# Cross-attention with sparsemax and a two-branch feed-forward: row normalisation on ScalarE, the 32-row tile's queries on column tiles, first loads from two queues, split relus, and a new emission order

## The chip, the cores and the metric

The kernel runs on one core of a Trainium2 chip. A core has TensorE (PE, matrix products; PEld is its weight load), VectorE (DVE), ScalarE (ACT), GpSimd (POOL) and SyncE (SP, which here only issues transfers). The engines run side by side, each through its own list of instructions in order, and wait for each other at semaphores. The metric is the device time of one execution in microseconds. The profile is of one further execution.

## The reference

Eight batches; each has 100 query rows of 512 numbers and a context of 722 rows. All is float32.

```
h   = layernorm(x)
q,k,v = h @ Wq + bq, ctx @ Wk + bk, ctx @ Wv + bv      # 16 heads of 32
s   = q k^T / sqrt(32)
att = sparsemax(s)          # max(s - tau, 0), with tau such that a row sums to 1
x   = x + (att v) @ Wo + bo
h2  = layernorm(x)
out = x + sqrt((h2 @ cos(theta + theta_noise))^2 + (h2 @ sin(phi + phi_noise))^2)
```

## The kernel before, in words

**Tiles.** The 800 query rows are cut into seven row tiles, `TILES = (128, 128, 128, 32, 128, 128, 128)`, across batch borders. The context comes transposed, 128 features by 722 positions, four slices a batch. Each float32 matmul stands in the trace as two records, so four matmuls are eight records.

**One batch.** Keys are four groups of 128 by 722, in halves of 361 columns (`keys`, L717; for batch 0 `keys_part`, L706, which works slice by slice as the loads come). ACT adds the bias (L728). A row tile is normalised: `stats` and `deviation` (L518 to L524), `normed` (L528, L530), transposed on PE (L538), copied (L544); `queries` (L554) makes q, four blocks of four matmuls. Scores are made in five fills of the one wide PSUM tile `psc` (`fill`, L800, on 32x32 array tiles; leftovers of four rows, L789, on column tiles). ACT copies each fill to SBUF (L811, two buffers `s_t`). DVE takes the eight largest of every segment of about 30 numbers (`tops`, L822, 312 MAX8 a batch), then builds 80 candidates per row (L831 to L849) and a first bound of the threshold (L857 to L879). Five Newton steps follow: a mask on DVE (`above`, L889), its product with the candidates on GpSimd (`above_values`, L894), a count and a sum on DVE (L900, L907, L908). GpSimd splits the threshold into three bfloat16 parts (`parts`, L929 to L946), PE transposes them (`parts_T`, L951), and `weights` (L995, L1008) makes q k minus the threshold again, transposed, five blocks a batch in the same `psc`. A relu (L1027, ACT; one half of one block on DVE, L1029) writes `aT`, and `outputs` (L1042, column tiles) multiplies with the values (`values`, L738; the last 82 rows L754, on column tiles). ACT adds the bias (L1056).

**A row tile's end.** When all rows of a tile have outputs: product with Wo (`product`, L612; for the last tile one product part per 128 features, L623; for the 32-row tile `small_product`, L580, which spreads the 512 columns over four column tiles), addition to x (L669), normalisation again, two products with the cosine and sine matrices (L612, L580; for the last tile in two column parts of 352 and 160, L638), squares and roots on ACT, sum and result on GpSimd (for the last tile on DVE, L655 and L663), store. GpSimd computes the angles (L488 to L502) during the first batches.

**Order.** The order on every engine is written out by a planner inside the kernel (class `Plan`). Each step is a task with an engine and a cost from the table `STEPS`; `hold` says which buffer a task takes and which tasks free it (`psc` one, `pm` four PSUM banks, `s` two, `x` three). `Plan.order` runs through the tasks as a list scheduler: on each engine the ready task that can start first, among those the one with the earliest due time. A due time is batch x `PERIOD` + `SHIFT` minus the length of the work behind it, plus `LAG` by kind and `NUDGE` by kind and batch; these are tables of numbers. On PE a task of the same array shape as the last is preferred by `STAY`. The tasks are then emitted in order of their planned start.

**Loads.** SP issues all loads, in plan order: first Wk and context slices in pairs, then x, Wq and the rest. 32 small matmuls (`warm_up`, L512) run on PE before the first load is in.

## Time and profile before

| | us |
|---|---|
| median of 3 runs (lowest, highest) | 591.64 (591.51, 592.07) |
| the profiled execution | 594.34 |
| its span, first to last instruction | 592.6 |
| PE busy | 580.5 |
| DVE busy | 517.3 |
| ACT busy | 261.8 |
| POOL busy | 224.2 |
| mean granted PE clock | 0.995 |
| PE waiting for the last row normalisation's copy, at 579.76 | 0.68 |

In the page, the digits of "PE", "DVE" and so on are the busy tenths of forty slices of 14.8 us. "PEclk" is the clock that the array was granted. In a row of a group, what follows the first bar is the busy time in sum and the mean of one in nanoseconds, and what follows the second is the engine's idle time just before, with what ended it. In the rows in order of time, the first number is the start, the second the length, and a bracket holds an idle time and what ended it.

### The profile page before, as it was taken

The numbers are of one execution on the slowest core, as the hardware profiler recorded it, in microseconds if no ns is written. First come the engines' busy times: TensorE is split into PE (matmuls) and PEld (weight loads), VectorE is DVE, ScalarE is ACT, GpSimd is POOL, SyncE is SP. The second block draws the span as 40 slices with busy tenths as digits, with TensorE's granted clock in tenths as the row PEclk, the third lists the DMA queues.
The fourth block names the chain that finished last, engine by engine and source line by source line (L and its number), as shares of the span: only waits on it lengthen the run. The fifth ranks groups of instructions, "written<-read, shape, count | busy, mean of one in ns | idle before, by whom it ended". The sixth has DMA issues, their size and how long they took to land.

```text
span 592.6 us, 18085 instructions
## 1 busy us (share of the span) xinstructions
PE 580.5 (98%) x6937; PEld 339.1 (57%) x6937; DVE 517.3 (87%) x3186; ACT 261.8 (44%) x399; POOL 224.2 (38%) x293
## 2 busy tenths in 40 slices
PE   9999999999999999999999999999999999999995
PEld 6655554567456743677457744576557544664553
DVE  3299999998999879998999899999999899999521
ACT  1353352455346523654345434363545534552532
POOL 1686799974400232004620232015200446045402
PEclk9999999999999989999999999999999999999999
DMA  8940300310011000200100002030000001000001
GB/s 323 316 136 20 118 19 19 108 49 2 19 35 70 2 1 2 102 3 20 43 2 3 2 2 101 3 102 2 3 2 2 14 25 59 3 20 1 3 2 39
DMA packets 12475, 26.61 MB, mean 45 GB/s; under 512 B 1872, under 2 KB 2128, under 8 KB 12384
## 3 DMA queue, kind: packets, MB, share of 16 engines
q1 hardware_dynamic: 11952, 24.03, 12.4%
q8 instruction: 56, 0.92, 0.6%
q0 software_dynamic: 432, 1.38, 0.6%
q14 instruction: 35, 0.29, 0.2%
HBM read 23.76 MB, written 1.64 MB: 43 GB/s over the span
## 4 chain that ended last, share of the span: by engine, by line
PE 60%; DVE 32%; POOL 4%; ACT 2%; issue 1%; DVEq 0%; POOLq 0%; ACTq 0%
PE pm L717 18%; DVE cand L822 15%; PE pm L738 10%; PE psc L1008 5%; PE pm L612 5%; PE pm L1042 4%; PE psc L800 4%; PE pm L554 3%; DVE f L907 3%; DVE m L889 3%; POOL p L894 2%; DVE n L900 2%; PE pm L754 2%; PE psc L706 2%; PE psc L995 2%; DVE rest L831 1%
## 5 line engine op out<-in xcount | busy, mean ns | idle before, releaser
L822 DVE MAX8 cand<-s_t 128x8 f32<-128x30 f32 x2496 | 230.7, 171 | 1.4 <-ACT s_t L811 1.4
L894 POOL TENSOR_TENSOR p<-z,m 128x1040 f32<-128x1040 f32 (+2 forms) x50 | 88.7, 1778 | 266.7 <-DVE m L889 261.8
L717 PE MATMUL pm<-c_t,wk_sb 128*128 128x361 f32 x464 | 152.5, 474 | 0.0
L738 PE MATMUL pm<-wv_sb,c_t 128*128 128x512 f32 x320 | 144.3, 598 | 0.0
L717 PEld LDWEIGHTS pm<-c_t,wk_sb 128*128 128x128 f32 x464 | 84.1, 189 | 53.8 <-issue 10.8
L738 PEld LDWEIGHTS pm<-wv_sb,c_t 128*128 128x128 f32 x320 | 58.5, 190 | 66.7 <-issue 65.6
L811 ACT COPY s_t<-psc 128x1924 f32<-128x1924 f32 (+2 forms) x40 | 69.1, 1726 | 50.1 <-DVE cand L822 30.0
L1027 ACT ACTIVATE aT<-psc 128x2000 f32<-128x2000 f32 (+2 forms) x38 | 66.5, 1749 | 53.2 <-PE pm L1042 36.2
L767 ACT COPY v_t<-pm 128x512 f32<-128x512 f32 x40 | 23.4, 586 | 85.1 <-PE pm L738 85.1
L907 DVE TENSOR_REDUCE f<-p 128x13 f32<-128x1040 f32 (+2 forms) x50 | 50.4, 1009 | 10.6 <-POOL p L894 10.5
L728 ACT ACTIVATE k_t<-pm,bk_sb 128x361 f32<-128x361 f32 x60 | 33.5, 562 | 55.8 <-PE pm L717 55.7
L900 DVE TENSOR_REDUCE n<-m 128x13 f32<-128x1040 bf16 (+2 forms) x50 | 50.3, 1007 | 0.6
L1008 PE MATMUL psc<-q_t,k_t 32*128 32x100 f32 (+1 forms) x1536 | 47.4, 264 | 0.0
L1008 PEld LDWEIGHTS psc<-q_t,k_t 32*128 32x128 f32 (+1 forms) x1536 | 46.4, 180 | 0.4
L800 PE MATMUL psc<-k_t,q_t 32*32 32x481 f32 (+1 forms) x1536 | 43.3, 474 | 0.8 <-ACT s_t L811 0.7
L1042 PE MATMUL pm<-aT,v_t 128*32 128x100 f32 (+1 forms) x1440 | 39.2, 251 | 0.1
L1042 PEld LDWEIGHTS pm<-aT,v_t 128*32 128x32 f32 (+1 forms) x1440 | 30.9, 109 | 7.1 <-issue 3.3
L554 PEld LDWEIGHTS pm<-hT,wq_sb 128*128 128x128 f32 x224 | 27.1, 191 | 6.3 <-issue 5.4
L554 PE MATMUL pm<-hT,wq_sb 128*128 128x128 f32 (+1 forms) x224 | 29.6, 280 | 0.0
L800 PEld LDWEIGHTS psc<-k_t,q_t 32*32 32x32 f32 x1536 | 14.0, 103 | 26.2 <-issue 19.4
L754 PE MATMUL pm<-wv_sb,c_t 128*18 128x128 f32 (+1 forms) x384 | 23.6, 311 | 0.0
L831 DVE MAX8 rest<-cand 128x8 f32<-128x120 f32 x104 | 20.1, 268 | 0.2
(307 smaller groups left out, 615.6 us busy)
## 6 DMA issues: line engine op xcount, KB each, us to landing
c_t<-in_ctx SPq DMA_DIRECT2D x7, 1444.0 KB, 6.6
x_t<-in_x SPq DMA_DIRECT2D x12, 256.0 KB, 3.1
c_t<-in_ctx SPq DMA_DIRECT2D x4, 361.0 KB, 5.1
out<-sq POOLq DMA_DIRECT2D x5, 256.0 KB, 2.8
wk_sb<-in_L_xattn_Wk SPq DMA_DIRECT2D x4, 256.0 KB, 4.6
wq_sb<-in_L_xattn_Wq SPq DMA_DIRECT2D x4, 256.0 KB, 5.7
cos_sb<-in_L_ffn_theta SPq DMA_DIRECT2D x4, 256.0 KB, 4.5
n_t<-in_L_ffn_theta_noise SPq DMA_DIRECT2D x4, 256.0 KB, 3.1
```

Source lines behind the costliest of these rows:

```text
L554: nc.tensor.matmul(tk["pq"][:, g, : tk["n"]], lhsT=wq_sb[:, c, g * P : (g + 1) * P], rhs=tk["hT"][:, c, :], start=(c == 0), stop=(c == NG ...
L717: nc.tensor.matmul(pk, lhsT=wk_sb[:, c, g * P : (g + 1) * P], rhs=st["c"][:, c, i * SH : (i + 1) * SH], start=(c == 0), stop=(c == NG - 1),)
L738: nc.tensor.matmul(pv, lhsT=st["c"][:, k, c * CK : (c + 1) * CK], rhs=wv_sb[:, k, :], start=(k == 0), stop=(k == NG - 1),)
L800: nc.tensor.matmul(psc[b * HD : (b + 1) * HD, j, at : at + EDGE[hi] - EDGE[lo]], lhsT=st["q"][r, g, qb * HD : (qb + 1) * HD], rhs=st["k"][ ...
L811: nc.scalar.copy(s_t[:, :, :n], st["psc"][:, :, :n])
L822: nc.vector.max(st["cand"][:, n, k, :], st["s", f][:, j, at + EDGE[k] - first : at + EDGE[k + 1] - first],)
L894: nc.gpsimd.tensor_tensor(st["p"][:, lo:hi], st["z"][:, lo:hi], st["m"][:, lo:hi], ALU.mult)
L900: nc.vector.tensor_reduce(n_t, st["m"][:, lo:hi], AX.X, ALU.add)
L907: nc.vector.tensor_reduce(s_t, st["p"][:, lo:hi], AX.X, ALU.add)
L1008: nc.tensor.matmul(psc[:m, j, k * Q : (k + 1) * Q], lhsT=st["k"][r, g, lo : lo + m], rhs=st["q"][r, g, :], start=False, stop=(k == len(PAI ...
L1027: nc.scalar.activation(a, b, AF.Relu, scale=SCALE)
L1042: nc.tensor.matmul(st["po", g][j * HD : (j + 1) * HD, :Q], lhsT=st["v"][:m, c, f : f + HD], rhs=aT[j][:m, j, k * Q : (k + 1) * Q], start=( ...
```

## The change

Five things change in what is computed where. (1) `normed` no longer runs on DVE: DVE keeps the reciprocal (`inverse`), ACT negates the mean, multiplies it by the reciprocal and writes the rows with one activation that scales and shifts. (2) The 32-row tile's queries are made by `small_product` on column tiles, copied into columns of its x tile, and turned by one transpose. (3) The first pair of loads is cut in four, weights issued by ACT and context by SP; the keys of the first slice run the first half of the context before the second; the bias bo is loaded early (its due time, in the tables). (4) In the last batch every relu is split, two heads on ACT and two on DVE, into two buffers. (5) The last 160 columns' addition runs on GpSimd. Twelve warm-up matmuls fewer. The losses are computed ahead of the first bound. The planner's costs and rules change a little, and its tables `SHIFT`, `LAG` and `NUDGE` are other numbers (left out here), so that the order on all engines is another.

In the order that results, PE has between two blocks of weights, in most batches, first a key block and then the outputs, where before most often the outputs came first and then the key block; the leftovers' fill stands inside the weights of the batch before in several batches; and the products with the cosine and sine matrices of the last tile but one stand between the last output product and the last normalisation.

```diff
-WARM = 32
+WARM = 20
...
-    "load x": ("SP", 0.7),
+    "load x": ("SP", 0.85),
+    "load first": ("SP", 1.3),
-    "deviation": ("ACT", 0.25),
-    "normed": ("DVE", 0.72),
+    "deviation": ("ACT", 0.45),
+    "inverse": ("DVE", 0.12),
+    "normed": ("ACT", 0.85),
...
+    "small queries": ("PE", 0.95),
+    "small copy": ("ACT", 0.33),
+    "small T": ("PE", 0.15),
...
+    "last result": ("POOL", 0.1, 0.0026),
...
-SHAPE = {"fill": 1, "fill last": 2, "outputs": 2, "small product": 2, "values last": 2, "weights": 3}
+SHAPE = {"fill": 1, "fill last": 2, "outputs": 2, "small product": 2, "small queries": 2, "values last": 2, "weights": 3}
-STAY = 70.0
+STAY = 145.0
+STAY_TILED = 50.0
-PERIOD = 121.0
+PERIOD = 126.0
...
-    LATENCY = {"PE": 0.25, "SP": 2.0}
+    LATENCY = {"PE": 0.25, "SP": 2.6}
...
                 for t in waiting:
...
-                        stay = STAY if engine == "PE" and t.shape == shape else 0.0
+                        stay = 0.0
+                        if engine == "PE":
+                            stay = STAY if t.shape == shape else STAY_TILED if t.shape and shape else 0.0
...
-                late = self.LATENCY.get(t.engine, 0.2)
-                n.ready = max(n.ready, t.end + (0.0 if n.engine == t.engine == "SP" else late))
+                late = 0.0 if n.engine == t.engine else self.LATENCY.get(t.engine, 0.2)
+                n.ready = max(n.ready, t.end + late)
...
-        x_t = rows.tile([P, DM], FP, name="x_t", bufs=3)[:n]
-        nc.sync.dma_start(x_t, rows_of_x)
+        x_t = rows.tile([P, DM], FP, name="x_t", bufs=3)
+        nc.sync.dma_start(x_t[:n], rows_of_x)
...
+    def load_first(st, b):
+
+        st["c"] = big.tile([P, NG, S], FP, name="c_t")
+        for i in range(2):
+            w_cols = slice(P, DM) if i else slice(0, P)
+            nc.scalar.dma_start(wk_sb[:, 0, w_cols], wk[:P, w_cols])
+            keys_i = slice(i * SH, (i + 1) * SH)
+            nc.sync.dma_start(st["c"][:, 0, keys_i], ctxT[b, :P, keys_i])
+
     def load_pair(st, b, c):
-        if c == 0:
-            st["c"] = big.tile([P, NG, S], FP, name="c_t")
...
+        nc.scalar.activation(tk["mv"][:, 0:1], tk["mv"][:, 0:1], AF.Copy, scale=-1.0)
+
+    def inverse(tk):
+        tk["rs"] = small.tile([P, 1], FP, name="rs")[: tk["n"]]
+        nc.vector.reciprocal(tk["rs"], tk["sd"])
     def normed(tk):
-        rs = small.tile([P, 1], FP, name="rs")[: tk["n"]]
-        nc.vector.reciprocal(rs, tk["sd"])
+        shift = tk["mv"][:, 0:1]
+        nc.scalar.activation(shift, shift, AF.Copy, scale=tk["rs"])
...
-        nc.vector.tensor_scalar(
-            tk["h"], tk["x"], tk["mv"][:, 0:1], rs, ALU.subtract, ALU.mult
-        )
+        nc.scalar.activation(tk["h"], tk["x"], AF.Identity, bias=shift, scale=tk["rs"])
...
+    def small_copy(tk):
+        tk["qs"] = tk["x whole"][:, :P]
+        nc.scalar.copy(tk["qs"], tk["pq"])
+
+    def small_T(tk):
+
+        pt = ps1.tile([P, NG, P], FP, name="pm")
+        nc.tensor.transpose(pt[:, 0, :], tk["qs"], ident)
+        tk["pq"] = pt[:, 0, :].rearrange("p (g t) -> p g t", g=NG)
+
     def small_residual(tk):
...
-    def half_result(tk, h):
+    def half_result(tk, h, engine):
...
-        nc.vector.tensor_tensor(a, a, tk["x"][:, half_of(h)], ALU.add)
+        engine.tensor_tensor(a, a, tk["x"][:, half_of(h)], ALU.add)
...
-        for n in range(EARLY):
-            g, i = divmod(n, 2)
+        for i, g in sorted((n % 2, n // 2) for n in range(EARLY)):
...
-    def once(fn):
-        return add("load bias", fn)
-
     def set_x(tk):
...
-        tk["x"] = load_x(x.rearrange("b q d -> (b q) d")[at : at + n], n)
+        tk["x whole"] = load_x(x.rearrange("b q d -> (b q) d")[at : at + n], n)
+        tk["x"] = tk["x whole"][:n]
...
-        h = add("normed" + two, lambda: normed(tk), d)
+        i = add("inverse", lambda: inverse(tk), d)
+        h = add("normed" + two, lambda: normed(tk), i)
...
-        hold("x", tk["x in"], [h])
-        qs = [add("queries", lambda g=g: queries(tk, g), hT, *w["q"]) for g in range(NG)]
-        hold("hT", hT_in, qs)
-        for g in range(1, NG):
-            plan.edge(qs[g - 1], qs[g])
+        if tk["n"] == HD:
+            pq = add("small queries", lambda: small_product(tk, "pq", "hT", wq_sb), hT, *w["q"])
+            cp = add("small copy", lambda: small_copy(tk), pq)
+            qs = [add("small T", lambda: small_T(tk), cp)]
+            hold("hT", hT_in, [pq])
+            hold("pm", pq, [cp])
+            hold("x", tk["x in"], qs)
+        else:
+            hold("x", tk["x in"], [h])
+            qs = [add("queries", lambda g=g: queries(tk, g), hT, *w["q"]) for g in range(NG)]
+            hold("hT", hT_in, qs)
+        for before, q in zip(qs, qs[1:]):
+            plan.edge(before, q)
...
-        tk["q first"] = qs[0]
+        tk["q first"] = pq if tk["n"] == HD else qs[0]
...
-            rz = add("half result", lambda h=h: half_result(tk, h), rt, tiles=z - a)
+            rz = add(
+                "last result" if h else "half result",
+                lambda h=h: half_result(tk, h, nc.gpsimd if h else nc.vector), rt, tiles=z - a,
+            )
...
-            for c in range(NG):
+            c_in.append(add("load first", lambda st=st, b=b: load_first(st, b)))
+            for c in range(1, NG):
...
-            w["bk"] = once(lambda: nc.sync.dma_start(bk_sb, bk))
+            w["bk"] = add("load bias", lambda: nc.sync.dma_start(bk_sb, bk))
...
-            w["bq"] = once(lambda: nc.sync.dma_start(bq_sb, bq))
-            w["bo"] = once(lambda: nc.sync.dma_start(bo_sb, bo.partition_broadcast(P)))
+            w["bq"] = add("load bias", lambda: nc.sync.dma_start(bq_sb, bq))
+            w["bo"] = add("load bo", lambda: nc.sync.dma_start(bo_sb, bo.partition_broadcast(P)))
...
-            w["bv"] = once(lambda: nc.sync.dma_start(bv_sb, bv.rearrange("(g p) -> p g", p=P)))
+            w["bv"] = add("load bv", lambda: nc.sync.dma_start(bv_sb, bv.rearrange("(g p) -> p g", p=P)))
         else:
...
-        for lo, hi in ((0, HG + 1), (HG + 1, 2 * HG + 1), (2 * HG + 1, NT)) if b == B - 1 else ((0, NT),):
+        spans = ((0, HG + 1), (HG + 1, 2 * HG + 1), (2 * HG + 1, NT)) if b == B - 1 else ((0, NT),)
+        for lo, hi in spans:
...
-            t = add("first bound", lambda st=st, r=r: first_bound(st, **r), cd, tiles=hi - lo)
...
+            if hi == NT:
+                ls = add("losses", lambda st=st: losses(st), *cds, *rest_steps)
+            t = add(
+                "first bound", lambda st=st, r=r: first_bound(st, **r), cd, *([ls] if hi == NT else ()),
+                tiles=hi - lo,
+            )
...
-            if b == B - 1 and n == len(PAIRS) - 1:
+            if b == B - 1:
...
-                            st, n, not k, slice(0, 2) if k else slice(2, HG), k
+                            st, n, (n + k) % 2 == 0, slice(0, 2) if k else slice(2, HG), k
...
-                        f, tiles=len(pairs),
+                        f, *top_steps, tiles=len(pairs),
...
-                    for k in (True, False)
+                    for k in (1, 0)
...
-                takes = {"aT": es[0], "s": es[1]}
+                takes = {"aT": es[n % 2], "s": es[1 - n % 2]}
             else:
-                spare = b == B - 1 and n % 2 == 1
-                es = [
-                    add(
-                        "weights relu", lambda st=st, n=n, spare=spare: weights_relu(st, n, spare), f,
-                        *(top_steps if spare else ()), tiles=len(pairs),
-                    )
-                ]
-                takes = {"s" if spare else "aT": es[0]}
+                es = [add("weights relu", lambda st=st, n=n: weights_relu(st, n), f, tiles=len(pairs))]
+                takes = {"aT": es[0]}
             hold("psc", f, es)
```

## The prediction

> **What bounds the kernel now.** I read the page first (busy shares, slices), then the chain that ended last, then TensorE alone in order of time, then the groups by shape.
>
> ```profile
> PE 580.5 (98%) x6937; PEld 339.1 (57%) x6937; DVE 517.3 (87%) x3186; ACT 261.8 (44%) x399; POOL 224.2 (38%) x293
> ...
> PE   9999999999999999999999999999999999999995
> ...
> PEclk9999999999999989999999999999999999999999
> ...
> PE 60%; DVE 32%; POOL 4%; ACT 2%; issue 1%; DVEq 0%; POOLq 0%; ACTq 0%
> ```
>
> TensorE (PE) is never free from 4.8 us, when the keys begin, to 587. Only less work for it, fewer waits or a better clock can shorten the span. The chain runs through VectorE (DVE) for a third of the time because DVE hands each batch's threshold over just in time: before the transposes of batches 0 and 6 PE stood 0.12 and 0.31 us, and in batch 1 the last part was ready 0.29 us ahead. So DVE is a second bound, close behind. The start, from the chain, columns start, length, what:
>
> ```profile
> 1.19 3.60 PE pm L512 x32
> 4.79 3.69 PE psc L706 x8
> ...
> 9.69 2.43 PE psc L706 x8
> ```
>
> The warm-up fills PE until 4.6 us; the first key slice and weights land at 3.71 and 4.65. Eight key records first take 3.69 us, later 2.43: until 6.9 us a record starts every 0.605 us, afterwards every 0.305. The array runs at half speed there, though the page's clock row does not show it. One later stretch, PE in order of time, then the granted clock of three windows (length, PE busy, PEclk, DMA, GB/s):
>
> ```profile
> 204.46 1.97 PE L554 MATMUL pm<-hT,wq_sb 128*128 128x32 f32 x16
> 206.36 0.90 PE L1042 MATMUL pm<-aT,v_t 128*32 128x100 f32 x32
> 207.19 1.08 PE L554 MATMUL pm<-hT,wq_sb 128*128 128x32 f32 x8
> 208.10 5.38 PE L612 MATMUL pm<-wo_sb,oT 128*128 128x512 f32 x8
> 213.32 0.97 PE L554 MATMUL pm<-hT,wq_sb 128*128 128x32 f32 x8
> ```
>
> ```profile
> 204.50:208.20 3.70, 3.70 (x61) 1.00 0.00 0
> 208.25:211.66 3.41, 3.41 (x6) 0.50 0.00 0
> ```
>
> The product at 208.10 takes 5.21 us to the next block; the same eight records take 3.44 elsewhere. It is no wait: the clock was halved for 3.41 us, just after the queries of the 32-row tile. Last, the places where PE waits near the end:
>
> ```profile
> 545.50 0.29 PE L951 MATMUL pm<-ident_b,t 128*128 128x128 bf16 x2 [1.14 <-POOL t L944]
> 558.74 1.07 PE L1042 MATMUL pm<-s_t,v_t 82*32 82x100 f32 x40 [1.16 <-ACT s_t L1027]
> 569.02 0.35 PE L995 MATMUL psc<-tT,neg_b 3*128 3x400 bf16 x4 [0.97 <-ACT s_t L1027]
> 579.76 2.63 PE L638 MATMUL pm<-cos_sb,hT 128*128 128x352 f32 x8 [0.68 <-ACT hT L544]
> ```
>
> With 0.70 at 94.7 us and small ones, PE's waits from 4.79 to 579.76 are 5.3 us.
>
> **The change part by part.** Each is priced on PE's path in the profiled execution (span 592.6 us, 594.34 with what lies around it). That execution is 2.7 us over the median of the runs, 591.64, so I subtract differences from the median.
>
> *Small queries on column tiles.* Removed: the four 32-column blocks, 1.90 + 0.91 + 0.81 = 3.62 us by their starts. Added: one small product, of which the trace has three (0.90, 0.99, 1.01), so 1.0; and one 128x128 transpose, a quarter of a 0.43 to 0.49 block of four, 0.11, with its drain 0.2. The copy between (128x128 on ScalarE, 0.26) lies beside a key block of 2.43 us. Net -2.4.
>
> *The clock dip.* The Trainium skill (TensorE: Matmul & The Clock Gate, What's actually happening) says that a monitor grants the clock by activity over free-running windows of 3.41 us. The dip lasted 3.41, and a window ending at 208.25 held mostly 32-column matmuls. By the row the change saves 5.21 - 3.44 = 1.77; by the rule the phase of the windows is chance, so runs without profile may not have had the dip, and the saving is 0. I take half, -0.9. The same rule speaks against the shorter warm-up: 20 matmuls at 0.107 end at 3.4 us, and if the pause until data arrives counts as idle, full speed comes a window later: 3.41 x 0.5 = 1.7 us lost. The old pause of 0.23 us did no harm; I take 0 and keep 1.7 for the range.
>
> *Start.* The first pair of loads becomes four, on SyncE and ScalarE at once. A 256 KB load issued at 0.88 landed at 3.71; the first needed parts (128 weight columns, half a context slice, 249 KB) should land alike, so keys begin at about 3.85, 0.94 earlier. If full speed still comes at 6.9, (6.9 - 3.85) / 0.605 = 5 records are slow rather than 3.5, and 1.5 x 0.3 = 0.45 goes back. Net -0.5, ends 0 and -0.95. The bo load (256 KB) now precedes pair 1, which landed at 6.99; at the 390 GB/s seen there that is 0.7 later, 7.7, and it is needed at 8.9: hidden, but 1.2 us is all the cover. The first x load moves behind all pairs on SyncE, from 9.32 to about 11.6 (0.66 for bo, 1.6 for pair 3); statistics of two tiles, deviation, reciprocal, shift and rows follow in 3 us, 14.6, and PE asks for them after 36 key records, at 16.3. Wq, four loads of 0.67 behind, is in by 16.5 and needed at 20.4.
>
> *Order and array shapes.* I summed PE's blocks in old and new order, each at its measured start-to-start time by kind and neighbour. Shape changes go from 215 to 219, about 0.1 each. A fill costs 0.62 where leftovers follow and 1.02 where a full-array block does; three more fills now precede a column-tiled block directly (-1.2, if values behave as leftovers do). With the last output product cut in four, net -0.5, ends +0.7 and -1.2.
>
> *Normalisation on ScalarE (ACT).*
>
> ```profile
> L530 DVE TENSOR_SCALAR h_t<-x_t,mv,rs 128x512 f32<-128x512 f32 x12 | 12.7, 1054 | 5.2 <-PE pm L538 4.6
> L679 ACT ACTIVATE sq<-sq 128x512 f32<-128x512 f32 x5 | 3.1, 629 | 3.0 <-POOL sq L676 3.0
> L524 ACT ACTIVATE sd<-mv,estepst 128x1 f32<-128x1 f32 x12 | 3.6, 297 | 17.4 <-DVE mv L520 17.4
> ```
>
> DVE loses 12 x 1.054 + 2 x 1.20 = 15.1 us; the reciprocal stays. It gains four half relus (0.99 for 800 columns, so 1.24 for 1000) and loses one result: 11 us less. ACT gains 14 x (2 x 0.297 + 0.63) = 17.1 and loses about 3.7 of relus. At 47% busy that is nothing by load. By position it costs nothing where PE has other work, and the last tile's chain (residual 0.69, statistics 0.87, deviation 0.29, reciprocal 0.16, shift 0.3, normalise 0.63, with hand-overs 3.5 us) now lies under two products of 3.43. Each wait of ACT for a reciprocal holds the key copies and relus behind it.
>
> *Split relus and waits.* Splitting lets the outputs start 1.25 rather than 1.84 us after the weights. Walking PE's new last blocks, outputs wait 0.35, 0.15 and 0.3 for the last three relus. The last of four product parts waits 0.54 for its bias (now nothing lies between; before, one part did), and the copy of the normalised rows costs 0.68 as before: 2.0 known. For hand-overs I add DVE's work to each last update against PE's to the transposes. They have 4 to 8 us in hand, except batch 2: its leftovers fill is placed at 184, its copy ends at 186, its MAX8 at 191; rests to last update take 36 us (37.9 in the old batch 1, 123.9 to 161.8), two checks, now ahead of the parts on GpSimd (POOL), 0.44, the parts 2.0: 229.4 against PE's 229.6. If they come later, the transposes wait, and all of PE behind them. I put 3.0 there and elsewhere in sum (ends 0.5 and 7). Waits 5.0 instead of 5.3: -0.3.
>
> *Tail.* The last 160 columns' addition goes to POOL: 1.267 us per 512 columns there, so 0.40, against 0.33 on DVE, and a hand-over: +0.15.
>
> Sum: -2.4 - 0.9 - 0.5 - 0.5 - 0.3 + 0.15 = -4.45; 591.64 - 4.45 = 587.2 us.
>
> **The rivals.**
> 1. *PE's smaller work shows almost whole*, 587.2; between 585 and 589.8 with the ends above. For: PE is busy everywhere and loses counted work; DVE gains 11 us of slack.
> 2. *More*: early full speed (-0.45 further), the dip whole (-0.9), hand-overs at 0.5 (-2.5) would give 583.4; a typical mix 584.2. Against: batch 2.
> 3. *The new order gives it back.* DVE's relief is not used, because fills come late to it (batch 2), and hand-overs cost 6.3 us rather than 3: 590.5. For: DVE stands behind fills in both orders; its actual batches ended 5 to 17 us after its own summed work. Against: PE in the old order hardly waited on this.
> 4. *Slower: ScalarE's queue becomes the bound.* A shift waits for a reciprocal that DVE reaches late; behind it stand relu and key copies, so the one wide psc tile stays taken and PE stops. Fourteen such places at 0.65 us each cost 9 us: 596. It decides against the change from 4.45 + 1.2 = 5.65 us, 0.4 us per place. For: ACT takes work in program order, and it already waited 17.4 us for statistics. Against: then it cost PE nothing.
>
> **How the numbers follow.** Chances 0.55, 0.12, 0.18, 0.15. A measurement of this kernel can tell about 0.2%, 1.2 us: 590.46 and 592.82 are the bounds. Case 1 and 2 are faster, case 3 half faster (0.09) with 0.07 inside and 0.02 slower, case 4 slower: 0.76, 0.07, 0.17. The likeliest time is case 1's, 587.2, with 585 to 589.8 its own. From 583.5 to 593 leaves out most of case 4 and the best of case 2, 0.17.
>
> **What would show it.** Keys begin near 3.85; queries of the small tile make one block of about 1 us and a transpose; no halved clock after it; PE busy about 575; DVE about 506, ACT about 275; PE's waits about 5, the largest before batch 2's transposes at about 229 or at the last outputs; half-width products starting near 575. Wrong would be: keys starting late or a second slow window, PE waiting for ACT behind a reciprocal, or hand-over waits above 7 us.

## The result, and the profile after

The changed kernel takes 594.63 us (median of 20 runs, 593.92 to 596.16) against 591.82 for the kernel before (20 runs beside it, 591.08 to 594.61): ratio 1.0042, interval 1.0032 to 1.0051. It is slower by 0.4%, where 0.8% faster was forecast; the time lies above the range. The profiled execution took 594.79 us, its span is 593.0.

The page's busy shares, PE's row by slices, and the shares of the chain that ended last:

```profile
PE 575.2 (97%) x6926; PEld 334.1 (56%) x6926; DVE 508.3 (86%) x3175; ACT 275.0 (46%) x442; POOL 222.7 (38%) x294
...
PE   7999999899999999999999999999999999999985
...
PE 50%; DVE 24%; POOL 12%; issue 9%; DMA 4%; ACT 0%; SPq 0%; POOLq 0%; ACTq 0%
```

The busy sums are near those of the prediction (PE 575, DVE 506, ACT 275). PE lost 5.3 us of work and the span did not shrink: so PE waits more. The places are in the other rows. GpSimd's part of the chain went from 4% to 12%, and the row of PE has a 7 at the start, an 8 in the eighth slice (104 to 119 us) and an 8 near the end.

PE in order of time, at the start and then its waits from 100 us on (0.68 at 545.60 and 0.46 at 570.60 are left out; a bracket is the wait and its releaser):

```profile
3.73 2.17 PE L751 MATMUL psc<-c_t,wk_sb 128*128 128x361 f32 x4 [0.22 <-DMA wk_sb<-in_L_xattn_Wk]
9.94 1.45 PE L751 MATMUL psc<-c_t,wk_sb 128*128 128x361 f32 x4 [1.60 <-DMA c_t<-in_ctx]
...
106.58 0.40 PE L996 MATMUL pm<-ident_b,t 128*128 128x128 bf16 x4 [1.51 <-POOL t L989]
110.46 1.10 PE L845 MATMUL psc<-k_t,q_t 32*32 32x481 f32 x31 [1.01 <-ACT s_t L856]
510.80 0.39 PE L1040 MATMUL psc<-tT,neg_b 3*128 3x500 bf16 x4 [1.05 <-ACT s_t L856]
...
560.18 0.28 PE L1087 MATMUL pm<-aT,v_t 128*32 128x100 f32 x2 [1.37 <-ACT aT L1072]
565.08 0.28 PE L1087 MATMUL pm<-s_t,v_t 128*32 128x100 f32 x2 [0.99 <-ACT s_t L1072]
569.24 0.28 PE L1087 MATMUL pm<-aT,v_t 128*32 128x100 f32 x2 [0.94 <-ACT aT L1072]
...
579.81 2.63 PE L684 MATMUL pm<-cos_sb,hT 128*128 128x352 f32 x8 [0.78 <-ACT hT L580]
```

Keys begin at 3.73, as forecast, and at 9.94 PE stands 1.60 us for the second pair of loads. From 106 us to the half-width products (the cosine product of the last tile's first 352 columns) at 579.81 the waits sum to 8.79 us, where the prediction had 5.0: four hand-overs of a batch (1.51, 1.01, 1.05, 0.68, in sum 4.25 for 3.0) and the last outputs and the last normalisation (1.37, 0.99, 0.94, 0.46, 0.78, in sum 4.54 for 2.0).

The small tile's queries, in the same view:

```profile
205.86 1.08 PE L616 MATMUL pm<-wq_sb,hT 128*32 128x128 f32 x32
...
209.40 0.27 PE L631 MATMUL pm<-ident,x_t 128*128 128x128 f32 x1
```

One block of 1.01 up to the start of the key block behind it and a transpose of 0.2: 1.21 for 3.62, the 2.4 us of the prediction. The granted clock is 1.00 from 205.9 to 213.0: no halved stretch follows.

The account from profile to profile, by the starts of PE's blocks. The kernel before without its one stretch of halved clock would start the half-width products at 577.99 and end at 590.8.

| | predicted | measured |
|---|---|---|
| start, to the first fill | -0.5 | +0.47 |
| small queries | -2.4 | -2.41 |
| other blocks (order, array shapes) | -0.5 | +0.2 |
| PE's waits | -0.3 | +3.53 |
| after the half-width products' start | +0.15 | +0.35 |
| sum | -3.55 | +2.15 |

The clock, the prediction's further -0.9, is not in the table. Most runs of the kernel before are near 591.8 and only 4 of the 20 near 594 (46 of 166 of those beside the experiments below, with a mean granted clock of 0.995), so its median does not pay for the halved stretch, and removing it saves the median nothing. The medians are 2.8 apart and not 2.15. The likely reason is the start: in the profiled execution of the kernel before, keys ran at half rate until about 6.9 us and the first fill started at 27.00; in that of b1_small_q below, whose start is the same and whose time of 591.5 is a usual one, half rate ended at 5.2 and the first fill started at 26.18. Against such an execution the start row is about +1.3.

The three groups of waits that matter each have rows that explain them. SyncE's queue in order of time, then the row of the bo load among the transfers (KB, and us from issue to landing):

```profile
1.79 0.42 SPq L1286 DMA_DIRECT2D bo_sb<-in_L_xattn_bo  x1
```

```profile
bo_sb<-in_L_xattn_bo SPq DMA_DIRECT2D x1, 256.0 KB, 6.5
```

Bo is one row of 2 KB, written to 128 partitions. It lands at 8.24; nothing else has landed since 4.6, and pair 1 (the second slice of Wk and of the context), issued right behind it, is in at 9.80. DVE and then ACT at the first block of the last batch's weights:

```profile
557.83 1.20 DVE L1074 TENSOR_SCALAR s_t<-psc 128x1000 f32<-128x1000 f32 x1 [0.30 <-PE psc L1053]
```

```profile
559.13 1.00 ACT L1072 ACTIVATE aT<-psc 128x1000 f32<-128x1000 f32 x1 [1.70 <-DVE s_t L1074]
```

The halves do not run side by side: ACT's begins when DVE's is over. And GpSimd during batch 0's Newton steps, then DVE waiting for it:

```profile
77.93 2.15 POOL L939 TENSOR_TENSOR p<-z,m 128x1040 f32<-128x1040 f32 x1
...
80.86 1.26 POOL L531 TENSOR_TENSOR cos_sb<-cos_sb,m_t 128x512 f32<-128x512 f32 x1
...
82.93 2.34 POOL L531 TENSOR_TENSOR cos_sb<-cos_sb,m_t 128x512 f32<-128x512 f32 x1
85.24 2.15 POOL L939 TENSOR_TENSOR p<-z,m 128x1040 f32<-128x1040 f32 x1
```

```profile
80.11 1.24 DVE L952 TENSOR_REDUCE f<-p 128x13 f32<-128x1040 f32 x1 [3.10 <-POOL p L939]
...
87.43 1.24 DVE L952 TENSOR_REDUCE f<-p 128x13 f32<-128x1040 f32 x1 [1.72 <-POOL p L939]
```

Two angle steps (5 us) stand between two of the products that DVE needs for the threshold, and 6.3 us of angle work (71.65 to 77.93) stood ahead of the first one shown. DVE waits 3.10 for that one, then 1.72, 2.49 and 1.03 for the next three. These four waits bring the end of the last update to 104.16, the parts to 106.5, and PE's two waits at 106.58 and 110.46.

### The profile page after: what moved, and what is told of

It is laid out like the page before. It is cut to its first block, busy times and chain, and to the rows that moved or that the text cites. A ratio compares the mean times of both kernels' runs of the same rounds, so it can differ in the third digit from the quotient of the medians.

```text
span 593.0 us, 18092 instructions
## 1 busy us (share of the span) xinstructions
PE 575.2 (97%) x6926; PEld 334.1 (56%) x6926; DVE 508.3 (86%) x3175; ACT 275.0 (46%) x442; POOL 222.7 (38%) x294
## 4 chain that ended last, share of the span: by engine, by line
PE 50%; DVE 24%; POOL 12%; issue 9%; DMA 4%; ACT 0%; SPq 0%; POOLq 0%; ACTq 0%
PE pm L762 15%; PE pm L783 12%; DVE cand L867 10%; PE psc L1053 4%; PE pm L1087 4%; PE psc L845 4%; PE pm L658 3%; PE pm L590 3%; DVE m L934 3%; DVE f L952 3%; POOL cos_sb L531 3%; POOL p L939 2%; DVE n L945 2%; PE pm L799 2%; DMA n_t<-in_L_ffn_theta_noise 2%
## 5 line engine op out<-in xcount | busy, mean ns | idle before, releaser
L1072 ACT ACTIVATE aT<-psc 128x2000 f32<-128x2000 f32 (+3 forms) x38 | 64.8, 1706 | 52.6 <-PE psc L1053 44.5
L1087 PEld LDWEIGHTS pm<-aT,v_t 128*32 128x32 f32 (+1 forms) x1440 | 32.4, 109 | 22.2 <-issue 16.6
L1087 PE MATMUL pm<-aT,v_t 128*32 128x100 f32 (+1 forms) x1440 | 41.3, 251 | 2.3 <-ACT aT L1072 2.3
L551 DVE BATCH_NORM_STATS2 st<-x_t 128x6 f32<-128x512 f32 (+1 forms) x14 | 9.4, 674 | 17.6 <-DMA x_t<-in_x 17.5
L590 PE MATMUL pm<-hT,wq_sb 128*128 128x128 f32 x192 | 23.7, 279 | 0.0
L590 PEld LDWEIGHTS pm<-hT,wq_sb 128*128 128x128 f32 x192 | 22.2, 192 | 2.2 <-issue 1.4
```

The source lines that it names most:

```text
L590: nc.tensor.matmul(tk["pq"][:, g, : tk["n"]], lhsT=wq_sb[:, c, g * P : (g + 1) * P], rhs=tk["hT"][:, c, :], start=(c == 0), stop=(c == NG ...
L1072: nc.scalar.activation(a, b, AF.Relu, scale=SCALE)
L1087: nc.tensor.matmul(st["po", g][j * HD : (j + 1) * HD, :Q], lhsT=st["v"][:m, c, f : f + HD], rhs=aT[j][:m, j, k * Q : (k + 1) * Q], start=( ...
```

## The experiments

The theory after these rows: three waits cost the time, and each can be taken away alone. (A) bo ahead of pair 1, about 1.4 us. (B) the relu's halves in turn because both read one PSUM tile, about 2.9. (C) angle work ahead of batch 0's products on GpSimd, about 2.5. The rivals: that the parts themselves do not give what was counted (small queries, or ACT's normalisation holding its queue, case 4 of the prediction); and that the four-piece load or the shorter warm-up costs the start. A ratio below is against the kernel before on the same chip; a difference to the changed kernel is one of medians, 594.63. The kernel before has medians of 592.02 to 592.78 beside these runs, for 591.82 beside the changed kernel. So a difference of medians can be off by some tenths of a us, and the trace's own difference stands beside it where there is one. The edits are given shortened, some in words.

### Bo later, the relu whole, the relu in two tiles, products first

Four edits to the changed kernel, each for one cause.

```diff
+ tasks.remove(bo_task)                      # bo later: behind the load of bv
+ tasks.insert(index_of("load bv") + 1, bo_task)
```

> The changed kernel with one load moved: the broadcast of bo is issued after the bv load (where the old kernel had it) instead of ahead of pair 1; order of everything else as it was. Theory 1 (the bo broadcast holds up the key slices: nothing else lands between 4.4 and 8.2 us): pair 1 lands near 6.0 instead of 9.8, TensorE's 1.6 us wait at 9.9 is gone, the first fill begins near 25.9 instead of 27.5, and the time falls by about 1.6, to 593.0. Rival (VectorE's hand-overs bind afterwards, or the queue would be as full without bo): the first fill comes earlier or not, but the time stays within 0.5 of 594.6.

Measured: 593.38 us, ratio 1.0010 (0.9997 to 1.0024), 1.25 less than the changed kernel. PE at the start:

```profile
8.58 1.38 PE L751 MATMUL psc<-c_t,wk_sb 128*128 128x361 f32 x4
...
26.04 1.09 PE L845 MATMUL psc<-k_t,q_t 32*32 32x481 f32 x32
```

The wait at pair 1 is gone, the first fill starts at 26.04 for 27.47, and later blocks stand 1.4 earlier. Pair 1 landed at 8.13, later than I had put it, and nothing landed from 4.60 to 7.19 here either: part of the slow stretch is not bo's, and no run explains it. The profiled executions below repeat the comparison: in the six with bo in front pair 1 is in at 9.20 to 9.89 and the first fill starts at 26.9 to 27.6; in the six with bo behind, at 7.13 to 8.45 and 26.0 to 26.9. Cause A is shown, at about 2.0 us on the landing of pair 1 and 0.9 on the first fill, on the mean.

```diff
-  weights_relu(st, n, (n + k) % 2 == 0, slice(0, 2) if k else slice(2, HG), k)
+  weights_relu(st, n, n % 2 == 1) if k else nothing     # the last batch's relus whole, on ACT
```

> The changed kernel with the five relu pairs of the last batch undivided again, each whole on ScalarE; order of the other steps as it was. Theory 2 (the two halves run one after the other, 1.2 + 0.1 + 1.0 us, since the second waits for the first): a whole relu of 1.84 us lets the outputs start about 0.46 us sooner in three places where TensorE waits (1.37, 0.99 and 0.94), so 1.2 us less, 593.4. Rival (the halves overlap and the waits have another cause): the outputs start 0.6 us later at each place, 1.8 us more, 596.4.

Measured: 593.66 us, ratio 1.0016 (1.0005 to 1.0026). ACT at the first of these blocks:

```profile
557.75 1.84 ACT L1072 ACTIVATE aT<-psc 128x2000 f32<-128x2000 f32 x1 [0.46 <-PE psc L1053]
```

One relu of 1.84 us is over sooner than two halves in turn (1.20 + 0.1 + 1.00). The three waits are 0.97, 0.52 and 0.58 for 1.37, 0.99 and 0.94: splitting had cost 1 us.

```diff
-  st["psw"] = psc = ps4.tile([P, HG, 512], FP, name="psc")
+  st["psw"] = two tiles [P, 2, 512], "psw0" and "psw1"    # last batch only; each half of the relu reads one
```

> The changed kernel with the last batch's weights written to two PSUM tiles of two banks each instead of one tile of four; ScalarE reads one, VectorE the other; all else as it was. Theory 2 (the halves run in turn because both read one tile): both halves now start about 0.15 us after the weights, the outputs follow 1.4 us after them instead of 2.4, TensorE's waits of 1.37, 0.99 and 0.94 become 0.3, 0 and 0.1, and the time falls by 2.9, to 591.7. Rival (the two engines cannot read PSUM side by side whatever the tiles, or another wait takes over): starts stay 1.1 to 1.3 us apart, no change within 0.5 of 594.6.

Measured: 591.85 us, ratio 0.9985 (0.9974 to 0.9996), 2.8 less. DVE, then ACT, at the same place:

```profile
557.87 1.20 DVE L1088 TENSOR_SCALAR s_t<-psw 128x1000 f32<-128x1000 f32 x1 [0.33 <-PE psw L1063]
```

```profile
557.87 1.00 ACT L1086 ACTIVATE aT<-psw 128x1000 f32<-128x1000 f32 x1 [0.43 <-PE psw L1063]
```

Same data, as many banks of PSUM, same two engines: as two tiles the halves start together, the outputs start at 558.92, and the three waits are 0.10, 0 and 0. So the turn-taking is a semaphore that the program puts on a tile with two readers (ACT's start was released by DVE's end), not a limit of PSUM. The Trainium skill (PSUM — Partial Sum Buffer, PSUM bank collisions raise a hardware error) says that accesses of two engines to different banks at the same time run clean; the start at 557.87 on both agrees. Cause B is shown.

```diff
+ each "above values" task of batch 0 is moved right behind its "above" task   # on GpSimd
```

> The changed kernel with GpSimd's queue in batch 0 turned round: each product of values above the threshold (p, 2.15 us) goes ahead of the angle work that stood before it; no work is added or removed. Theory 3 (angle work ahead of p holds the threshold search: VectorE waits 3.1, 1.7, 2.5 and 1.0 us for p between 77 and 102): these waits fall to about 0.7 each, batch 0's last update comes some 5 us earlier than 104.2, TensorE's waits of 1.51 before the transposes at 106.6 and 1.01 before the fill at 110.5 vanish, and the time falls by 2.5, to 592.1. Rival (the place is made up later, since the hand-overs of the following batches bind anyway): those waits vanish but others appear, and the time stays within 0.7 of 594.6.

Measured: 593.98 us, ratio 1.0022 (1.0011 to 1.0033), only 0.65 less, inside what the rival had. DVE still waited 1.07, 1.73 and 4.56 for three products, and PE for the parts:

```profile
94.93 1.24 DVE L952 TENSOR_REDUCE f<-p 128x13 f32<-128x1040 f32 x1 [4.56 <-POOL p L939]
```

```profile
106.93 0.40 PE L996 MATMUL pm<-ident_b,t 128*128 128x128 bf16 x4 [1.79 <-POOL t L989]
```

The last update came at 102.6, and two angle steps then stood ahead of the parts. The 1.01 at the next fill went, the wait for the parts did not (1.79 for 1.51). The edit was too small to take the cause away, so this run left C open.

### Angle work: four more orders of one queue

All angle work of that stretch behind the parts:

```diff
+ the angle steps and noise loads between the first product and the parts of batch 0 are moved behind the parts
```

> The changed kernel with all angle work of GpSimd that stood between batch 0's first p and its parts (and the sines and noise loads that follow from it) moved behind these parts, in the same order; nothing added or removed. a4 had left an angle step ahead of the fourth p (wait 4.6) and two ahead of the parts. Theory 3, mended: VectorE's waits for p are about 0.7 each, batch 0's last update comes near 94 instead of 104.2, the parts by 97, both waits of TensorE at 106.6 and 110.5 (1.51 and 1.01) vanish, and the time falls by 2.5, to 592.1. Rival (a4's 0.65 is all there is: the later batches give it back): no more than 0.8 less, 593.8.

Measured: 608.51 us, ratio 1.0266 (1.0244 to 1.0287). The cosines on ACT need the angles, stand ahead of the copies of the next fills in ACT's program order, and waited 8.5 us. PE, and then the window that follows (length, PE busy with records, granted clock, DMA share, GB/s):

```profile
114.32 1.92 PE L845 MATMUL psc<-k_t,q_t 32*32 32x481 f32 x32 [10.78 <-ACT s_t L856]
```

```profile
114.30:117.70 3.40, 3.38 (x38) 0.50 0.02 5
```

This fill copy held everything, and PE came back to half a clock. The run with this order and three mends (bo later, two tiles, the last addition on DVE) has the same stop:

> The changed kernel with four mends at once: bo's load late, the last batch's weights on two PSUM tiles, the angle work behind batch 0's parts, the last 160 columns' addition back on VectorE. If the causes lie in different places of TensorE's row and add up: 1.25 + 2.8 + 2.5 + 0.2 = 6.7 less than 594.6, so 587.9, which would also be 0.6% faster than the kernel before. If VectorE's hand-overs bind as a whole (one mend only uncovers the next wait): no better than 590.

Measured: 605.40 us, ratio 1.0219 (1.0197 to 1.0241), with 10.77 us of PE's wait.

One angle step behind each product, the rest behind the parts:

```diff
+ window = [product, one angle step] x 4, product, parts, then the other angle steps
```

> The changed kernel with GpSimd's queue in batch 0 in the order p, one angle step, p, one angle step and so on, the parts right after the fifth p, and the left-over angle steps, the cosines on ScalarE and the checks after these. a9 had put the cosines on ScalarE and the noise load so that ScalarE waited 8.5 us with fill copies behind it; here one angle step (1.9 us) fits beside VectorE's own 3.1 us between two p. Theory 3: VectorE's waits for p are about 0.7 to 1.2 each, batch 0's last update comes near 96 instead of 104.2, both waits of TensorE at 106.6 and 110.5 vanish, and the time falls by 2.5, to 592.1. Rival (given back later): the two waits vanish, but later ones grow, and no more than 0.8 is gained, 593.8.

Measured: 597.66 us, ratio 1.0080 (1.0062 to 1.0097). DVE waited 1.06 and then 0.72 per step and its last update came at 99.3 for 104.16. But ACT, and then PE:

```profile
101.38 2.56 ACT L539 ACTIVATE cos_sb<-cos_sb,half_pi 128x512 f32<-128x512 f32 x4
```

```profile
105.64 1.10 PE L845 MATMUL psc<-k_t,q_t 32*32 32x481 f32 x32 [2.17 <-ACT s_t L856]
```

The fill's copy on ACT began at 103.84, behind the four cosines and the table load of 1.28 us that goes before them. They were ready at the moment when a fill's copy was due and ran ahead of it. At 109.5 us the order was 0.98 ahead of the changed kernel (0.58 of it from an earlier start in this execution), and it lost more than that later: 1.15 at 151 us, where a fill waited for queries that DVE wrote after a wait of 4.50 for batch 1's first product, 0.33 and 0.64 at 174, 0.62 at 212. With the three mends:

> Four mends in the changed kernel: bo's load late, the last batch's weights on two PSUM tiles, GpSimd's queue of batch 0 as in a10, the last 160 columns' addition back on VectorE. If the causes stand in different places of TensorE's row and add up: 1.25 + 2.8 + 2.5 + 0.2 = 6.7 less than 594.6, so 587.9 (0.7% faster than the kernel before). If VectorE's hand-overs take the place of what is mended: 590 or more.

Measured: 594.43 us, ratio 1.0021 (1.0010 to 1.0032), on the rival's side. The pause on PE at 105.69 is the same 2.17 as without the mends, but here the clock was halved after it. Two windows of PE of this run, then two of the run without the mends (columns as above):

```profile
103.15:106.56 3.41, 1.24 (x34) 1.00 0.00 0
106.56:109.97 3.41, 3.41 (x25) 0.50 0.02 5
```

```profile
101.14:104.55 3.41, 2.32 (x8) 1.00 0.00 0
104.55:107.96 3.41, 2.32 (x40) 1.00 0.02 5
```

Of the 22 runs 20 show a mean granted clock of 0.994 to 0.996 and take 593.5 to 595.9; the two at 0.998 take 592.4 and 592.6.

The same with the cosines moved behind, to 145 us:

```diff
+ a10's order, the three mends, and the cosines moved behind the last sines' task
```

> The kernel with three mends, and GpSimd's queue of batch 0 as in a10, but the cosines on ScalarE moved on to where the sines stand (145 us), so that they hold no fill copy; a10 had lost 2.2 us to that. Theory 3: TensorE's waits at 106 and 110 (2.5 together) vanish and nothing else grows: 2.5 less than the kernel with three mends, 587.9. Rival (a4 and a10: the next hand-over of VectorE, before the transposes at 172 to 174, gives it back): 0.5 to 1 less only, 589.6.

Measured: 594.16 us, ratio 1.0036 (1.0023 to 1.0049). Batch 0's waits were gone, 2.1 us by 107 us. Then batch 1's first product found angle work ahead of it. PE in order of time, then windows of PE (columns as above):

```profile
151.86 1.89 PE L847 MATMUL psc<-k_t,q_t 32*32 32x481 f32 x24 [3.19 <-DVE q_t L605]
```

```profile
150.00:152.00 2.00, 0.14 (x12) 0.75 0.00 0
152.00:154.00 2.00, 2.00 (x26) 0.50 0.00 0
```

A pause of 3.19 us, and from 151.0 to 157.8 the clock was halved, which costs about 3.0 us more (half of the time from 151.86 on): nearly a pause counted twice.

So cause C can be mended only if the angle work collides neither with the products of batch 0, nor those of batch 1, nor ACT's copies.

### The three mends without the angle work, and with it spread

```diff
+ bo behind the load of bv; two tiles for the last batch's weights
-  half_result(tk, h, nc.gpsimd if h else nc.vector)
+  half_result(tk, h, nc.vector)
```

> Three mends in the changed kernel, its order otherwise untouched: bo's load late (measured alone: 1.25), the last batch's weights on two PSUM tiles (2.8), the last 160 columns' addition on VectorE (0.2). If the causes stand in separate places of TensorE's row they add up: 4.25 less than 594.63, so 590.4, faster than the kernel before by 0.3%. If one uncovers another's wait: 591.5 or more.

Measured: 590.53 us, ratio 0.9967 (0.9954 to 0.9980). A and B and the addition on DVE together, as added up before the run.

```diff
+ a14, and: one angle step behind each of batch 0's first four products; five angle steps behind batch 1's parts;
+ the cosines behind a value copy of batch 2 (about 160 us), the last sines behind one of batch 3 (about 221 us)
```

> The kernel with three mends, and GpSimd's angle work spread out: one angle step after each of batch 0's p, the parts right after the fifth, the rest before batch 1's p, but the last chunk of sines' angles (8 us of GpSimd) only after batch 1's parts at 170, where GpSimd stood idle for 33 us; cosines and sines on ScalarE moved into gaps between value copies at 160 and 221. Theory 3 (the 2.5 us at 106 and 110 are GpSimd's angle work ahead of the threshold search, and a13 lost because the same work then stood ahead of batch 1's search): the waits at 106 and 110 vanish, batch 1's transposes and the queries do not wait, and the time falls by 2.1 to 2.5 against three mends, to 588.3. Rival (GpSimd has no room left, or VectorE's own row is the limit): waits of another 2 us turn up before 240, 590 or more.

Measured: 588.25 us, ratio 0.9927 (0.9908 to 0.9946). DVE, then PE, where the wait of 3.10 and those of 1.51 and 1.01 had been, and the shares of the chain:

```profile
76.63 1.24 DVE L954 TENSOR_REDUCE f<-p 128x13 f32<-128x1040 f32 x1 [1.06 <-POOL p L941]
...
98.27 0.17 DVE L955 SCALAR_TENSOR_TENSOR t0 0_1160<-f,n 128x13 f32<-128x13 f32 x1
```

```profile
103.56 0.40 PE L998 MATMUL pm<-ident_b,t 128*128 128x128 bf16 x4
```

```profile
PE 74%; DVE 22%; POOL 1%; issue 1%; DMA 1%; ACT 1%; ACTq 0%; POOLq 0%
```

The last update ends at 98.44 for 104.16, both waits of PE are gone (the transposes at 103.56, and the next fill at 106.37, start without one), and GpSimd's share of the chain goes from 12% to 1%. Cause C is shown, at 2.3 us (590.53 - 588.25; the two runs are from two chips on which the kernel before has 592.02 and 592.08). This version beats both kernels.

### The parts alone, on the kernel before

Only the small queries:

```diff
+ g == 0: one small product into a pm tile, copied;  last g: one transpose of the copy
```

> The kernel before with the small tile's queries alone on column tiles (one product of 32 rows, a copy on ScalarE, one transpose at the place of its fourth query block), the order of all other steps as it was. My step: four blocks of 3.62 us become 1.2, so 2.2 to 2.4 less, 589.5, and no halved clock after them. Rival (VectorE hands over just in time in that stage, so TensorE only waits instead): within 0.5 of the kernel before.

Measured: 591.61 us, ratio 0.9992 (0.9980 to 1.0004): nothing that can be told. PE:

```profile
206.59 0.90 PE L1066 MATMUL pm<-aT,v_t 128*32 128x100 f32 x32 [1.79 <-ACT aT L1051]
```

In the old order the 32-column blocks stood between a block of weights and its outputs and covered the relu. Taken away, PE waits 1.79 for it. In the new order key work stands there, and the 2.41 of the table are whole. The gain is one of both parts together.

Only the normalisation on ACT:

```diff
-  nc.vector.tensor_scalar(tk["h"], tk["x"], tk["mv"][:, 0:1], rs, ALU.subtract, ALU.mult)
+  ACT: negate the mean, multiply by rs, Identity with bias and scale
```

> The kernel before with the normalisation alone on ScalarE (the negated mean, the shift and the rows as activations; the reciprocal stays on VectorE in its old place), order as it was. My step: 15 us less on VectorE, 17 more on ScalarE, nothing on TensorE's path; the time within 0.7 of the kernel before, rather below it. Rival (ScalarE's queue becomes the bound, since it waits for reciprocals with key copies and relus behind): 2 to 4.4 us more, 594 to 596.

Measured: 592.84 us, ratio 0.9998 (0.9984 to 1.0012).

```profile
PE 578.8 (98%) x6937; PEld 338.4 (57%) x6937; DVE 504.5 (85%) x3172; ACT 277.6 (47%) x441; POOL 222.7 (38%) x293
```

DVE 12.8 us less, ACT 15.8 more, the time the same. Case 4 of the prediction falls for the old order, and so does any gain from DVE's relief in it.

Only the first loads, the key order and 20 warm-up matmuls, with bo where it was:

```diff
-WARM = 32
+WARM = 20
+ load_first: weights in two pieces by ACT, context in two by SP; keys sorted by half, then group
```

> The kernel before with the start of the change alone: the first key slice and weights in four pieces on two queues, key parts in the new order, 20 warm-up products instead of 32; bo's load stays late. My step said 0.5 less, between 0 and 0.95: keys begin at 3.75 instead of 4.8 to 4.95, but the array runs at half speed until about 6. Expected now 0.2 to 0.5 less, 591.5. Rival (the shorter warm-up loses a window of full speed): 1.0 to 1.7 more, 593.

Measured: 592.99 us, ratio 1.0012 (1.0003 to 1.0022).

```profile
7.61 1.38 PE L711 MATMUL psc<-c_t,wk_sb 128*128 128x361 f32 x4
...
26.89 1.09 PE L805 MATMUL psc<-k_t,q_t 32*32 32x481 f32 x32
```

PE, at the block before which full rate comes and at the first fill. Keys start at 3.72, a microsecond earlier, and more of them run at half rate, until 7.6 here. The first fill starts at 26.89 for 27.00 in the profiled execution of the kernel before (26.18 and 26.99 in those of the two runs above, which keep the old start). So the first fill moves by between -0.1 and +0.7, and the interval of the ratio lies above 1: the early start buys nothing, and by the medians it costs 0.7 us (0.2 to 1.3). That is near the rival's 593, but no run here separates the 12 warm-up matmuls fewer from the loads in four pieces and the order of the keys, so which of them costs it stays open.

## Why the prediction was wrong, point by point

| cause, and the run that shows it | us |
|---|---|
| bo ahead of pair 1 (a1_bo_late: 594.63 - 593.38) | 1.25 |
| relu halves in turn (a6_two_tiles: 594.63 - 591.85) | 2.8 |
| angle work ahead of batch 0's products (590.53 - 588.25) | 2.3 |
| last addition on GpSimd (its store issued 8.87 for 8.63 after the half-width products' start; not run alone) | 0.2 |
| sum; 594.63 - 588.25 = 6.4 | 6.55 |

Without these the change stands at 588.25, 1.1 us above the 587.2 of the prediction. That it comes so near is in part luck: the -0.9 for the clock and the -0.5 for the start did not come, and PE's waits in that version are 3.1 us rather than 5.0.

*Start: failed.* The step that failed is "at the 390 GB/s seen there that is 0.7 later, 7.7 ... hidden". Two terms of it were too small. Bo put pair 1 back by 1.7 us (9.80 against 8.13 in a1_bo_late; 2.0 on the mean of six and six executions), not by 0.7: the load has 256 KB on its writing side and one row of 2 KB on its reading side, and I priced it by a neighbour of the same size. Its own row in the trace of before warned of this (it landed 3.74 us after the load ahead of it, at 33.76 for 30.02), though that gap is no price either: it is 0.46 to 0.56 in the six runs where bo stands behind a whole context. And pair 1 without bo lands at 8.13 in the new start, not at the 6.99 of the old one. So 1.2 us of cover stood against 2.8, and PE waits 1.60. The second step, five slow records for 3.5, did not hold: the end of the half rate differs from one execution to the next (below), and by b3_first the term is +0.7 (0.2 to 1.3), not -0.5. (The first parts are 64 + 180.5 = 244.5 KB, not 249; that changes nothing.)

*Split relus: failed, and the largest error.* The step is "outputs start 1.25 rather than 1.84 us after the weights". They start 2.4 to 2.5 after. The trace of before shows the one block that was already split, in the views of DVE and ACT:

```profile
570.32 0.99 DVE L1029 TENSOR_SCALAR s_t<-psc 128x800 f32<-128x800 f32 x1 [11.41 <-PE psc L1008]
```

```profile
571.41 0.84 ACT L1027 ACTIVATE aT<-psc 128x800 f32<-128x800 f32 x1 [2.21 <-DVE s_t L1029]
```

ACT starts when DVE ends and is released by it. I took the duration from the first row and did not look at the bracket of the second. So 0.8 us of known waits became 3.3 (1.37 + 0.99 + 0.94).

*Hand-overs: mechanism right, place wrong, size short.* "Batch 2 ... at about 229" had no wait (its transposes run at 232.6 without one). I had added DVE's work to each last update and GpSimd's only for batch 2; the queue of GpSimd in batch 0 was not walked, though GpSimd computes the angles in the first batches, as the kernel's description has it, and the order of the changed kernel could be read from its program. There four of the five products stood behind angle steps. 4.25 us for 3.0.

*Small queries: right,* 2.41 for 2.4, and 0 in the old order.

*The clock: the rule was right, the half was not.* The row gave 1.77, and the free-running windows of the page on the clock gate (the Trainium skill, TensorE: Matmul & The Clock Gate, What's actually happening) gave 0, since their phase is chance. Against a median it is 0. The profiled execution was 2.7 us above the median, and this told already that the dip was not in the median.

*Normalisation on ACT at nothing: right.* b2_act_norm moves 13 us of DVE and leaves the time, and in the changed kernel no wait of PE's names the normalisation ahead of the last one (0.78 for 0.68).

*Order and shapes:* +0.2 for -0.5, inside its ends (+0.7 and -1.2). *Tail:* +0.24 of the addition for +0.15; the other 0.1 is less than what the last store alone varies.

*The rivals.* Case 3, the order gives it back through hand-overs, is in part what happened (1.25 more than counted), but not through fills that come late to DVE. Case 4 is not seen. None had a relu that splitting makes longer, nor a load that costs three times its size's price; the case on the slower side was chosen on ACT, whose new work was the largest by sum, and the slower mechanisms were in the pieces that had looked free.

*Open:* the slow stretch of the transfers between 4.6 and 7.2 us, which the run with bo later and b3_first also have; which of its three parts makes b3_first slower; and which part of the later loss in the order with one step between comes from which queue. The waits of 1.05 at 510.80 and 0.68 at 545.60 are left in a15_spread too (1.05 and 0.69). The first goes through DVE: the fill's copy on ACT at 508.99 had waited 2.03 us for MAX8 on an earlier fill, which DVE did between the steps of the threshold search.

## What to carry to other kernels

Look up an operation that changes its place or its size by its own row in the trace before, not by a neighbour's, and read the bracket of that row as well as its length: both main errors had a warning in rows that were there. A gap between two landings is still not the price of the second load; what it costs shows in what stands behind it. An operation split over two engines is two only if the program lets both go at once; where one tile has two readers, see who releases the second. Where a new order comes with the change, walk every engine's queue between the first need and the last use, one batch after the other; relief of the bound engine buys nothing if another queue hands over the same thing later.

## What the runs showed of the hardware

- A load with one row of 2 KB for all 128 partitions (256 KB written) slowed the queue at the start: from 5 to 6 us the transfers moved 119 GB/s with it (changed kernel) and 284 with a plain load in its place (a1_bo_late). It landed 2.8 to 3.7 us after the load ahead of it there, and 0.46 to 0.56 in the six runs where a context of 1.4 MB stood ahead; plain loads of 256 KB in a steady stretch land 0.65 to 0.7 apart.
- Full rate at the start (records 0.305 us apart, not 0.605) came at 5.2 to 7.1 us with 32 warm-up matmuls and at 5.4 to 7.9 with 20: 4.0 to 6.7 us after the first matmul at 1.19. The Trainium skill (TensorE: Matmul & The Clock Gate, the section on what happens) gives half a microsecond either way; the spread here is wider. With three executions at 32 the traces cannot tell whether it depends on the number of warm-up matmuls.
- The halved stretches last 3.41, 6.83 and 13.65 us, one, two and four times 3.41. Whether a pause of PE halves the clock depends on where it falls: the same 2.17 us lay whole in the 3.41 us before 106.56 in a11_all, the order with one step between and three mends (PE busy 1.24 of them), and the next 3.41 were halved; in a10_angles_between, that order without the mends, with the grid of 3.41 counted from its first full rate at 5.57, it is split over two (2.32 busy in each), and nothing was halved. Pauses that filled 1.79 and 1.63 us of one such stretch (a4_p_first, products first; b1_small_q) halved nothing; 3.19 us gave two halved ones (a13_four, cosines moved), 10.78 gave four, two of them during the pause (a9_angles_late, all angle work behind the parts). Busy time by the records is not all of it: the halved stretch of the kernel before follows one in which PE was busy throughout, mostly with 32-column matmuls.
- From one execution to the next, the last store alone took between 2.8 and 3.8 us to land.
